# Edge rows for a 7x7 convolution: copied inside DRAM from the main rows instead of stored from the chip

## The chip, the core and the metric

The kernel runs on one core of a Trainium2 chip. A core has a matrix engine (TensorE, PE in the profile), a vector engine (VectorE, DVE), a scalar engine (ScalarE, ACT), a general engine (GpSimd, POOL) and a queue engine (SyncE, SP) that does little but issue transfers. The transfers themselves are moved by sixteen DMA engines that all queues share. The metric is the device time of one execution in microseconds (us), the median of several runs.

## What is computed

The input x has 384 channels of 192 x 192 numbers in float32. The reference is two layers:

```python
# layer 0
qkv = maxpool2x2(conv1x1(groupnorm(x), w_qkv))          # 1152 channels of 96 x 96
q, k, v = split(depthwise3x3(qkv))
attn = normalize(q) @ normalize(k).T * temperature      # 48 x 48 in each of 8 heads
out = sum(a_i * topk_softmax(attn, k_i) @ v)            # four values of k
x = x + conv1x1(upsample2x(gelu(out)), w_proj)
# layer 1
x = x + depthwise7x7(groupnorm(x), symmetrized weight)
```

The 7x7 convolution of layer 1 needs, for each output row, three rows above and three below it.

## The kernel before

The kernel runs in four stages: the statistics of the first norm, the q and k part with the sums for the attention matrix, the v part, and the 7x7 convolution. The change lies in the third, which also makes what the fourth reads.

**How the image is cut.** The 192 rows are six strips (`NT`) of 32 rows (`TR`). The v stage works on sixteen blocks (`NBC`); block b takes rows 2b and 2b+1 (`RB` = 2) of all six strips at once. The blocks are gone through in the order 13, 14, 15, 0, 1, 2 and so on (`order`, line 528), so that a block's neighbours are there in time.

**What the v stage leaves in DRAM.** The sum x + layer 0 is written channel by channel in a layout that suits the 7x7 stage: `sd` (line 115) has 4 x 32 rows of 384 channels, where a row is a run of 300 numbers (`RUN`): six strips of 50. The factor 4 (`CP`) splits the columns by their remainder modulo 4. `sh` (line 117) has 64 more rows of the same shape: the edge rows. For each of the three rows above and below a strip it holds ten shifted views (`NQ` = 10), which the 7x7 stage reads as further rows of its matrix product, 30 for above, 30 for below. Each edge row equals, but for a shift of a strip (50 numbers, `JP`) or of one column, a main row in `sd`: rows 29, 30 and 31 of the strip before, or rows 0, 1 and 2 of the strip behind.

**The loop of the v stage** (lines 1137 to 1164) runs for i = 3 to 15. One pass does, for v's block i, nine products `convolve` (line 542: six products of TensorE each, then a maximum on DVE), reading image rows `xv` that `load_v` (line 933) brings in three groups of three transfers on SyncE's queue; and for block j = i - 2 it finishes the depthwise taps, applies the attention (`attend`), projects (`project`, line 1031) and adds the input (`residual`, line 1062), whose image rows `xr` come through `load_r` (line 1054), three transfers on the same queue. The buffer `xvs` of image rows exists once: a group is loaded again when the last product that reads it is over, which gives each load a lead of most of a block. The order of the products and of most work on DVE is fixed by hand (`keep`); the order of the transfers on SyncE's queue is not, and is chosen when the program is built.

**The stores.** `residual` builds two rows of 128 channels in one of three buffers `sx`. For each of the two rows it issues on GpSimd's queue one store to `sd` (line 1117), and, if the row is one of the six that lie at a strip's edge, three stores to `sh` (line 1127: four, four and two of the ten views). Rows 29 to 31 and 0 to 2 come in blocks 14, 15, 0 and 1, that is in the passes i = 3 to 6: 9, 18, 18 and 9 stores.

**The 7x7 stage** reads `sd` and `sh` through `load_main` and `load_aux` (line 1257). Its first reads of `sh` are issued at 2173.5 us of the profile.

Of the kernel before, what the change touches and what calls it, by code (L numbers as in the profile page):

```python
# [14 lines left out]
C = 384  # L15
# [44 lines left out]
TR = 32  # L60
NT = HW // TR
CP = 4
NJ = HW // CP
JP = NJ + 2
RUN = NT * JP
HALO = KS // 2
NQ = CP + KS - 1
LEAD = JP + 2


TOP = 32
BOT = 64
# [5 lines left out]
RB = 2  # L78
# [4 lines left out]
CB = 8  # L83
# [3 lines left out]
def conv_preact_d2(  # L87
# [17 lines left out]
    nc = tc.nc  # L105
# [9 lines left out]
    sd = dram.tile([CP * TR, C, RUN], F32, name="sd")  # L115

    sh = dram.tile([SHR, C, RUN], F32, name="sh")
# [177 lines left out]
    with tc.tile_pool(name="stp", bufs=1) as stp, tc.tile_pool(name="xsp", bufs=5) as xsp:  # L295
# [149 lines left out]
        for b in [*range(NB - 2, NX, -2), NX, *reversed(range(NX))]:  # L445
            n = 2 if b > NX else 1
# [88 lines left out]
    def image_rows(ct, b, t0, nt):  # L535
        return bass.AP(
            x.tensor,
            x.offset + (ct * P * HW + t0 * TR + b * RB) * HW,
            [[HW * HW, P], [TR * HW, nt], [1, RB * HW]],
        )  # L540

    def convolve(i, t0, ct, xb, pin):
        b, rows = order[i], place(i)
        o = (2 * KT + ct) * P
        ps = pv.tile([P, UT, 512], F32, name=f"pv{b}_{t0}_{ct}", tag="pv")
        for u in range(UT):
            for kt in range(KT):
                pin(
                    nc.tensor.matmul(  # L549
                        ps[:, u, 0 : RB * HW], wq[:, kt, o : o + P], xb[:, u, kt, :],  # L550
                        start=(kt == 0), stop=(kt == KT - 1),
                    )
                )
        pin(
            nc.vector.tensor_reduce(  # L555
                rows[ct][:, 1 + t0 : 1 + t0 + UT, 1 : PS + 1],
                ps[:, :, 0 : RB * HW].rearrange("p u (a w b) -> p u w a b", a=2, b=2),
                AX.XY,
                ALU.max,
            )  # L560
        )

    with ExitStack() as bx:
# [55 lines left out]
        with tc.issue_after(loaded):  # L619
            for kt in range(KT):  # L620
                cs = slice(kt * P, (kt + 1) * P)
# [137 lines left out]
        for b in range(NB + 1):  # L759
# [11 lines left out]
            for ct in range(2 * KT + 1):  # L771
# [12 lines left out]
                if b > 0 and ct > 0:  # L784
# [5 lines left out]
                    flat = dst.rearrange("p h w -> p (h w)")  # L790
# [142 lines left out]
    def load_v(i, t0):  # L933
        xb = xvs[:, t0 : t0 + UT]
        for kt in range(KT):
            nc.sync.dma_start(xb[:, :, kt], image_rows(kt, order[i], t0, UT))
        return xb
# [4 lines left out]
    def depthwise_v(i, ct, dys, pin=lambda ins: ins):  # L942

        b = order[i % NBC]
        if (i, ct) not in vbs:
            tag = f"vlast{i}" if i >= NBC - 1 else "vb"
            vbs[i, ct] = vp.tile(
                [P, NT, PS], F32, name=f"vb{i}_{ct}", tag=tag, bufs=KT if i >= NBC - 1 else 2 * KT
            )
        dst = vbs[i, ct]  # L950
        for dy in dys:
            r = b + dy - 1
            t0 = 1 + r // NBC
            rows = place(i + dy - 1)[ct]
            for j in range(3):
                src = rows[:, t0 : t0 + NT, j : j + PS]
                w = wd[:, 2 * KT + ct, 3 * dy + j : 3 * dy + j + 1]
                if (i, ct) in begun:
                    pin(nc.vector.scalar_tensor_tensor(dst, src, w, dst, ALU.mult, ALU.add))  # L959
                else:  # L960
                    begun.add((i, ct))
                    pin(
                        nc.vector.tensor_scalar(
                            dst, src, w, bdb[:, 2 * KT + ct : 2 * KT + ct + 1], ALU.mult, ALU.add
                        )
                    )


    AHEAD = 3
# [55 lines left out]
    sdv = sd.rearrange("(v r) c n -> r c v n", v=CP)  # L1025
# [28 lines left out]
    def load_r(i, ot):  # L1054

        if i == NBC - 1:
            return xvs[:, :, ot]
        xr = xp2.tile([P, NT, RB * HW], F32, name=f"xr{order[i % NBC]}_{ot}", tag="xr")
        nc.sync.dma_start(xr, image_rows(ot, order[i % NBC], 0, NT))
        return xr  # L1060

    def residual(i, ot, y, xr, pin):

        b = order[i % NBC]
        flat = sxs[(i * KT + ot) % len(sxs)]
        xq = xr.rearrange("p t (a j e) -> p a t j e", a=RB, e=CP)

        def at(e):

            return LEAD + (e + CP - 1) % CP * RB * RUN + int(e > 0)  # L1070


        for e, f in ((1, 2), (0, 3)):
            for a in range(RB):
                pin(
                    nc.vector.tensor_tensor(  # L1076
                        bass.AP(
                            flat.tensor, flat.offset + at(e) + a * RUN,
                            [flat.ap[0], [JP, NT], [1, NJ], [at(f) - at(e), 2]],
                        ),  # L1080
                        xq[:, a, :, :, e : f + 1 : f - e],
                        y,
                        ALU.add,
                    )
                )
            yield
        if i == 1:

            m = mid1[:, ot : ot + 1]
            nc.vector.tensor_tensor(m, ysum[:, ot, b, 0:1], ysum[:, ot, b, 1:2], ALU.add)  # L1090
            nc.vector.tensor_scalar_mul(m, m, 1.0 / PBC)
            nc.vector.tensor_tensor(m, m, chmean[:, ot : ot + 1], ALU.add)
            nc.vector.tensor_scalar_mul(negmid[:, ot : ot + 1], m, -1.0)
        for k, (e, f) in enumerate(((1, 2), (3, 0))):
            pin(
                nc.scalar.activation(  # L1096
                    junk,
                    bass.AP(
                        flat.tensor, flat.offset + at(e),
                        [flat.ap[0], [at(f) - at(e), 2], [JP, RB * NT], [1, NJ]],  # L1100
                    ),
                    AF.Square, bias=negmid[:, ot : ot + 1], accum_out=sqsum[:, ot, b, k : k + 1],
                )
            )
            if k == 0:
                yield
        cs = slice(ot * P, (ot + 1) * P)

        def rows_of(a, nv, shift):
            o = LEAD + a * RUN + shift  # L1110
            return bass.AP(
                flat.tensor, flat.offset + o, [flat.ap[0], [RB * RUN, nv], [1, RUN]]
            )

        for a in range(RB):
            r = b * RB + a
            nc.gpsimd.dma_start(sdv[r, cs], rows_of(a, CP, 0))  # L1117

            halos = []
            if r >= TR - HALO:  # L1120
                halos.append(((r - TR + HALO) * NQ, -JP))
            if r < HALO:
                halos.append((BOT - TOP + r * NQ, JP))
            for h, shift in halos:
                for q in range(0, NQ, CP):
                    nv = min(CP, NQ - q)
                    nc.gpsimd.dma_start(
                        sh[h + q : h + q + nv, cs].rearrange("f c n -> c f n"),
                        rows_of(a, nv, shift + q // CP),
                    )  # L1130


    spare = [(NBC, ct, dy) for ct in range(KT) for dy in (1, 2)]
# [3 lines left out]
    for i in range(AHEAD, NBC):  # L1137
        j = i - 2
        xb = load_v(i, 0)
        for ct in range(KT):  # L1140
            depthwise_v(j, ct, (2,), keep)
            convolve(i, 0, ct, xb, keep)
        gl = attend(j)
        xb = load_v(i, UT)
        for ct in range(KT):
            depthwise_v(i - 1, ct, (0, 1), keep)
            if ct == 1:
                convolve(i, UT, 0, xb, keep)
        convolve(i, UT, 1, xb, keep)
        if spare[i - AHEAD]:  # L1150
            depthwise_v(*spare[i - AHEAD][:2], spare[i - AHEAD][2:], keep)
        convolve(i, UT, 2, xb, keep)
        ys = [project(j, ot, gl) for ot in range(KT)]
        xb = load_v(i, 2 * UT)
        sums = [residual(j, ot, ys[ot], load_r(j, ot), dve_keep) for ot in range(KT)]
        for ot in range(2):
            for _ in sums[ot]:
                pass
        convolve(i, 2 * UT, 0, xb, keep)
        next(sums[2])  # L1160
        convolve(i, 2 * UT, 1, xb, keep)
        for _ in sums[2]:
            pass
        convolve(i, 2 * UT, 2, xb, keep)
# [7 lines left out]
    for j in range(NBC - 2, NBC + 1):  # L1172
        gl = attend(j, keep)
        after = []
        for ot in range(KT):
            for _ in before[ot]:
                pass
            y = project(j, ot, gl, keep)
            after.append(residual(j, ot, y, load_r(j, ot), keep))
            next(after[ot])  # L1180
            next(after[ot])
            if (j, ot) == (NBC - 2, 1):
                for ct in range(KT):
                    depthwise_v(NBC, ct, (0,), keep)
        before = after
# [13 lines left out]
    with ExitStack() as ex_:  # L1199
# [258 lines left out]
        for n in range(steps):  # L1458
# [33 lines left out]
            for q in range(CP):  # L1492
                ps = sums(q, range(2 if q in ahead else 0, 3))
                c = n * CB + 2 * q
# [16 lines left out]
            if n in later:  # L1511
                ps = pc.tile([P, 2, 512], F32, name=f"al{later[n]}", tag="pc")
                for i, dg in enumerate(dgs):
                    cs = slice(i * P, (i + 1) * P)
# [63 lines left out]
```

## Time and profile before

The time is 2763.55 us, the median of 3 runs (2759.44 to 2763.87). The profiled execution took 2784.9 us at a mean granted TensorE clock of 0.985.

| engine | busy, us | share of the span |
|---|---|---|
| PE (products) | 2591.1 | 93% |
| PE weight loads, beside the products | 1525.2 | 55% |
| DVE | 2456.2 | 88% |
| ACT | 1140.1 | 41% |
| POOL | 746.7 | 27% |

| DMA queue | what it carries | MB | share of 16 engines |
|---|---|---|---|
| q1 (SyncE and others) | x, xv, xr, output | 283.44 | 29.0% |
| q0 (GpSimd) | sd, sh, weights of the 7x7 stage | 148.85 | 15.8% |
| q10 (ACT) | inputs of the 7x7 stage | 147.07 | 14.1% |

A share is an average over the whole span, while the stages differ much: the core's DMA moved 34 to 40 GB/s in parts of the q and k stage and 372 GB/s in most of the 7x7 stage. What a change in the v stage is worth must be read from that stage. It begins to load residual rows at 1360 us, its edge rows are stored from 1488.6 to 1679.2 us, and its last store to `sd` is issued at 2197 us. The page gives the time in 40 slices of 69.6 us; a finer table of stretches and the list of waits are shown with the prediction.

### The profile page before, as it was taken

The numbers are of one execution on the slowest core, as the hardware profiler recorded it, in microseconds if no ns is written. First come the engines' busy times: TensorE is split into PE (matmuls) and PEld (weight loads), VectorE is DVE, ScalarE is ACT, GpSimd is POOL, SyncE is SP. The second block draws the span as 40 slices with busy tenths as digits, with TensorE's granted clock in tenths as the row PEclk, the third lists the DMA queues.
The fourth block names the chain that finished last, engine by engine and source line by source line (L and its number), as shares of the span: only waits on it lengthen the run. The fifth ranks groups of instructions, "written<-read, shape, count | busy, mean of one in ns | idle before, by whom it ended". The sixth has DMA issues, their size and how long they took to land. (4 is left out here: it accounts for less than half of the span.)

```text
span 2784.9 us, 25837 instructions
## 1 busy us (share of the span) xinstructions
PE 2591.1 (93%) x8365; PEld 1525.2 (55%) x8365; DVE 2456.2 (88%) x3527; ACT 1140.1 (41%) x2262; POOL 746.7 (27%) x885
## 2 busy tenths in 40 slices
PE   0399999999999999999899969999999899999998
PEld 0144444444444444444556646666666677777776
DVE  7989998989999999999789958999889789888886
ACT  0143423333343333433402312232323577777776
POOL 1024443100000000000111321010101478787876
PEclk9999999999999999999899989999999999999999
DMA  9976766301010110110336997566674899999998
GB/s 381 402 252 217 249 213 228 130 34 68 35 68 35 40 62 35 68 35 0 120 103 238 340 362 231 192 230 219 203 246 151 324 343 366 372 375 372 372 374 264
DMA packets 234039, 581.01 MB, mean 209 GB/s; under 512 B 16640, under 2 KB 165744, under 8 KB 217136
## 3 DMA queue, kind: packets, MB, share of 16 engines
q1 hardware_dynamic: 173408, 283.44, 29.0%
q0 software_dynamic: 37376, 148.85, 15.8%
q10 hardware_dynamic: 23120, 147.07, 14.1%
q8 instruction: 67, 1.10, 0.2%
q14 instruction: 68, 0.56, 0.1%
HBM read 370.93 MB, written 208.21 MB: 208 GB/s over the span
## 5 line engine op out<-in xcount | busy, mean ns | idle before, releaser
L663 PE MATMUL pq<-xq,wq 128*128 128x512 f32 x2268 | 1028.8, 597 | 5.4 <-DVE ring L673 4.7
L708 DVE SCALAR_TENSOR_TENSOR qk<-ring,wd,qk 128x384 f32<-128x384 f32 x1152 | 699.4, 616 | 59.5 <-ACT ring L695 32.1
L663 PEld LDWEIGHTS pq<-xq,wq 128*128 128x128 f32 x2268 | 408.7, 190 | 437.3 <-issue 364.0
L549 PE MATMUL pv<-xv,wq 128*128 128x384 f32 x1656 | 545.7, 490 | 26.0 <-DMA xv<-in_x_dram 21.7
L549 PEld LDWEIGHTS pv<-xv,wq 128*128 128x128 f32 x1656 | 316.7, 192 | 245.8 <-issue 20.4
L1482 PE MATMUL pc<-main,w 128*128 128x288 f32 x1536 | 436.4, 406 | 3.0 <-PE al L1515 1.7
L1502 DVE TENSOR_SCALAR apart<-pc,rb 32x576 f32<-32x576 f32 x384 | 312.1, 813 | 81.2 <-PE pc L1482 55.4
L1482 PEld LDWEIGHTS pc<-main,w 128*128 128x128 f32 x1536 | 290.6, 190 | 87.1 <-issue 2.4
L725 ACT COPY qkT<-turns 32x288 f32<-32x288 f32 x768 | 329.0, 428 | 20.7 <-DVE turns L791 9.3
L1500 ACT ACTIVATE apart<-pc,rb 32x576 f32<-32x576 f32 x384 | 281.1, 732 | 133.5 <-PE pc L1482 128.7
L959 DVE SCALAR_TENSOR_TENSOR vb<-rows,wd,vb 128x576 f32<-128x576 f32 x384 | 313.3, 817 | 11.3
L673 DVE TENSOR_REDUCE ring<-pq 128x128 f32<-128x512 f32 x428 | 292.1, 683 | 3.7 <-PE pq L663 3.6
L1482 PE MATMUL pc<-aux,h 128*128 128x288 f32 x768 | 248.1, 405 | 0.0
L719 ACT ACTIVATE junk<-qk 128x384 f32<-128x384 f32 x144 | 71.1, 494 | 411.8 <-DVE qk L708 411.0
L1441 POOL COPY res<-apart 128x1152 f32<-128x1152 f32 (+1 forms) x96 | 222.0, 2338 | 13.3 <-ACT apart L1500 9.5
L826 POOL TENSOR_TENSOR rn<-rn,halfpos 128x6 f32<-128x6 f32 x1 | 1.4, 1359 | 827.5 <-DVE rn L825 827.5
L1076 DVE TENSOR_TENSOR sx<-xr,y 128x576 f32<-128x576 f32 x180 | 203.8, 1173 | 19.9 <-ACT y L1047 14.8
L555 DVE TENSOR_REDUCE rows<-pv 128x192 f32<-128x768 f32 x144 | 137.7, 957 | 84.7 <-PE pv L549 84.6
L1117 POOL DMA_DIRECT2D sd<-sx x96 | 72.2, 755 | 514.5 <-DVE sx L1076 493.2
L741 PEld LDWEIGHTS grams<-qkT,qkT 128*96 128x96 f32 x576 | 92.8, 165 | 147.3 <-issue 136.1
L1096 ACT ACTIVATE wq<-sx,negmid 128x1152 f32<-128x1152 f32 x96 | 120.6, 1257 | 122.5 <-DVE sx L1076 118.2
L1482 PEld LDWEIGHTS pc<-aux,h 128*128 128x128 f32 x768 | 145.1, 189 | 41.2 <-issue 0.2
(227 smaller groups left out, 2270.6 us busy)
## 6 DMA issues: line engine op xcount, KB each, us to landing
sd<-sx POOLq DMA_DIRECT2D x96, 600.0 KB, 10.1
out_dram<-res SPq DMA_DIRECT2D x192, 288.0 KB, 11.2
main<-sd ACTq DMA_DIRECT2D x46, 1200.0 KB, 6.7
xv<-in_x_dram SPq DMA_DIRECT2D x138, 384.0 KB, 6.6
xr<-in_x_dram SPq DMA_DIRECT2D x45, 1152.0 KB, 11.7
xq<-in_x_dram SPq DMA_DIRECT2D x21, 2304.0 KB, 8.2
w<-wt ACTq DMA_DIRECT2D x46, 1024.0 KB
xs<-in_x_dram SPq DMA_DIRECT2D x24, 1536.0 KB, 15.1
```

Of the source, the lines that this page charges most:

```text
L549: nc.tensor.matmul(ps[:, u, 0 : RB * HW], wq[:, kt, o : o + P], xb[:, u, kt, :], start=(kt == 0), stop=(kt == KT - 1),)
L555: nc.vector.tensor_reduce(rows[ct][:, 1 + t0 : 1 + t0 + UT, 1 : PS + 1], ps[:, :, 0 : RB * HW].rearrange("p u (a w b) -> p u w a b", a=2, ...
L663: ins = nc.tensor.matmul(ps, wq[:, kt, ct * P : (ct + 1) * P], rows[:, kt, :, g * 64 : (g + 1) * 64], start=(kt == 0), stop=(kt == KT - 1) ...
L673: nc.vector.tensor_reduce(t[:, r0 : r0 + PR, 1 + g * 32 : 1 + (g + 1) * 32], ps.rearrange("p (h a w b) -> p h w a b", h=PR, a=2, b=2), AX. ...
L708: nc.vector.scalar_tensor_tensor(dst, src, w, dst, ALU.mult, ALU.add)
L725: nc.scalar.copy(side[f * Q : (f + 1) * Q].rearrange("p c (t n) -> p t c n", n=P)[:, :, :, a * Q : (a + 1) * Q], turns[a * Q : (a + 1) * Q ...
L959: pin(nc.vector.scalar_tensor_tensor(dst, src, w, dst, ALU.mult, ALU.add))
L1076: nc.vector.tensor_tensor(bass.AP(flat.tensor, flat.offset + at(e) + a * RUN, [flat.ap[0], [JP, NT], [1, NJ], [at(f) - at(e), 2]],), xq[:, ...
L1441: keep(copy(res[ps, k], apart[ps, :, k].rearrange("p e n -> p n e")))
L1482: nc.tensor.matmul(ahead[q][:, k, 0 : NT * NJ], lhs, rhs, start=(j == 0), stop=(j == 2), skip_group_check=True,)
L1500: keep(nc.scalar.mul(dst, src, scale))
L1502: keep(nc.vector.tensor_scalar_mul(dst, src, scale))
```

## The change

The stores of edge rows (`rows_of` and the loop over `halos`) go. What is stored to `sd` stays as it is. A list `edges` has the 18 transfers that fill `sh`: six rows by three groups of views (4, 4 and 2). Each is a copy from `sd` to `sh` for all 384 channels, on SyncE's queue. `copy_edge` issues the next of them. It is called behind the three groups of `xv` loads of a pass, from pass i = 7 on: two in each pass and a third in odd passes, until the list is empty. The purpose is to take the edge rows out of the passes in which they are all made at once, and to spread them over later passes.

```diff
         cs = slice(ot * P, (ot + 1) * P)
-        def rows_of(a, nv, shift):
...
         for a in range(RB):
-            r = b * RB + a
-            nc.gpsimd.dma_start(sdv[r, cs], rows_of(a, CP, 0))
-
-            halos = []
-            if r >= TR - HALO:
-                halos.append(((r - TR + HALO) * NQ, -JP))
-            if r < HALO:
-                halos.append((BOT - TOP + r * NQ, JP))
-            for h, shift in halos:
-                for q in range(0, NQ, CP):
-                    nv = min(CP, NQ - q)
-                    nc.gpsimd.dma_start(
-                        sh[h + q : h + q + nv, cs].rearrange("f c n -> c f n"),
-                        rows_of(a, nv, shift + q // CP),
-                    )
+            nc.gpsimd.dma_start(
+                sdv[b * RB + a, cs],
...
+            )
+    edges = [
+        (f + h * NQ + q, r + h, shift + q // CP, min(CP, NQ - q))
+        for f, r, shift in ((0, TR - HALO, -JP), (BOT - TOP, 0, JP))
+        for h in range(HALO)
+        for q in range(0, NQ, CP)
+    ]
+
+    def copy_edge(now):
+        if not now or not edges:
+            return
+        f, r, shift, nv = edges.pop(0)
+        n = CB * RUN
+        nc.sync.dma_start(
+            sh[f : f + nv].rearrange("f (a c) n -> f a (c n)", c=CB),
+            bass.AP(
+                sd.tensor, sd.offset + r * C * RUN + shift,
+                [[TR * C * RUN, nv], [n, C // CB], [1, n]],
+            ),
+        )
...
         xb = load_v(i, 0)
+        copy_edge(i > AHEAD + 3)
...
         xb = load_v(i, UT)
+        copy_edge(i > AHEAD + 3)
...
         xb = load_v(i, 2 * UT)
+        copy_edge(i > AHEAD + 3 and i % 2)
```

More of the change, by code (lines that the diff above doesn't have):

```diff
@@ L1107, in residual @@
         cs = slice(ot * P, (ot + 1) * P)
-        def rows_of(a, nv, shift):
-            o = LEAD + a * RUN + shift
-            return bass.AP(
-                flat.tensor, flat.offset + o, [flat.ap[0], [RB * RUN, nv], [1, RUN]]
-            )
-        for a in range(RB):
-            r = b * RB + a
-            nc.gpsimd.dma_start(sdv[r, cs], rows_of(a, CP, 0))
-            halos = []
-            if r >= TR - HALO:
-                halos.append(((r - TR + HALO) * NQ, -JP))
-            if r < HALO:
-                halos.append((BOT - TOP + r * NQ, JP))
-            for h, shift in halos:
-                for q in range(0, NQ, CP):
-                    nv = min(CP, NQ - q)
-                    nc.gpsimd.dma_start(
-                        sh[h + q : h + q + nv, cs].rearrange("f c n -> c f n"),
-                        rows_of(a, nv, shift + q // CP),
-                    )
+        for a in range(RB):
+            nc.gpsimd.dma_start(
+                sdv[b * RB + a, cs],
+                bass.AP(
+                    flat.tensor, flat.offset + LEAD + a * RUN,
+                    [flat.ap[0], [RB * RUN, CP], [1, RUN]],
+                ),
+            )
+    edges = [
[11 more added lines that the diff above has]
+            sh[f : f + nv].rearrange("f (a c) n -> f a (c n)", c=CB),
+            bass.AP(
+                sd.tensor, sd.offset + r * C * RUN + shift,
+                [[TR * C * RUN, nv], [n, C // CB], [1, n]],
+            ),
+        )
     spare = [(NBC, ct, dy) for ct in range(KT) for dy in (1, 2)]
```

## The prediction

> **What bounds the kernel now.** I read the page first (section 2, then the sums of section 1), then the table of stretches, then who waited for whom, then the order of time around the one hole. The chain of waits is of no use here: it was followed only over the last microsecond or so before the end. Section 2 of the page, 40 slices of 69.6 us each:
>
> ```profile
> PE   0399999999999999999899969999999899999998
> DMA  9976766301010110110336997566674899999998
> ```
>
> TensorE (PE) is at nine tenths in all slices but a few, and the change lies in slices 21 to 31 (1460 to 2230 us), the stage that makes v, attends, projects and stores. There one slice falls to 6, number 23, right where the DMA row reads 9 9. So the stage is TensorE's except at one place. The stretches between the issues of the first residual load of each block show what a block costs (columns: length, then busy time of PE, weight loads, DVE, ACT and POOL, then clock, DMA share, GB/s):
>
> ```profile
> 1490.30:1539.60 49.30, 49.30 (x169) 31.84 (x169) 45.50 (x61) 15.00 (x32) 11.91 (x16) 1.00 0.92 315
> 1539.60:1589.00 49.40, 49.40 (x170) 31.94 (x169) 44.91 (x53) 13.76 (x30) 18.06 (x24) 1.00 1.02 356
> 1589.00:1660.70 71.70, 53.19 (x175) 33.01 (x173) 49.63 (x55) 18.77 (x40) 23.82 (x32) 0.87 1.03 364
> 1660.70:1714.50 53.80, 50.61 (x163) 32.38 (x164) 40.37 (x48) 8.76 (x20) 3.70 (x5) 0.92 0.65 214
> 1714.50:1763.90 49.40, 49.40 (x170) 31.94 (x169) 45.01 (x52) 13.77 (x30) 4.48 (x6) 1.00 0.66 219
> ```
>
> An undisturbed block is 49.4 us of unbroken TensorE, with the DMA engines at 0.65 and 219 GB/s. While edge rows are stored the DMA share rises to 1.0. The third and fourth stretch together are 125.5 us, which is 26.7 us over two blocks. That is all that the edge stores cost today. What ended the waits from 1440 to 1720 us (total, times, longest):
>
> ```profile
> PE pv L549 <- DMA xv<-in_x_dram: 21.7, 3, 15.9
> ```
>
> So TensorE stood 21.7 us for image rows whose loads queued behind saturated DMA; the other 5 us are the lower clock after the stand (0.87 and 0.92). The DMA answer gives the transfers of one block and those to be replaced (KB each, median us to landing):
>
> ```profile
> sd<-sx POOLq DMA_DIRECT2D x96, 600.0 KB, 10.1
> xv<-in_x_dram SPq DMA_DIRECT2D x138, 384.0 KB, 6.6
> xr<-in_x_dram SPq DMA_DIRECT2D x45, 1152.0 KB, 11.7
> sh<-sx POOLq DMA_DIRECT2D x36, 600.0 KB, 16.2
> sh<-sx POOLq DMA_DIRECT2D x18, 300.0 KB, 16.0
> ```
>
> [...] an xv load, 6.6 us at the median, needed up to 38.6 us while the Pool queue was full of stores.
>
> **The change, part by part.**
>
> 1. 54 stores of edge rows leave the Pool queue (36 of 600 KB, 18 of 300 KB: 27.65 MB). On Pool they are 54 x 0.75 us = 41 us of issue, worth nothing: Pool is 27% busy and waits for DVE. On the DMA engines they are 27.65 MB at the 367 GB/s that the saturated window 1580 to 1630 us shows, 75 us of all sixteen, in four blocks. The middle two carried 10.8 + 9.2 = 20 MB each, 54 us of DMA in a block of 49.4. Their removal takes away the hole: **minus 26.7 us**.
>
> 2. 18 copies join the SyncE queue, in which all xv and xr loads of this stage stand. The source asks for 4 (or 2) rows of 48 pieces, but the built instruction carries a pattern of 4 x 8 x 14400 numbers (2 x 8 x 14400 for the six small ones): slowest dimension 4 or 2. [...] Either way each of these moves 460.8 KB: one whole row of 384 x 300 numbers. [...]
>
> 3. Cost of one copy on such an engine. No DRAM to DRAM transfer of this size is in the trace. Nearest row: the page's best slice moved 402 GB/s, 25.1 GB/s an engine: 460.8 KB take 18.3 us. [...] For the upper end I let reading and writing the same memory cost 20% more, 22 us (an estimate). I take 18.3 us: 18 x 18.3 = 330 us.
>
> 4. Where they lie. In the changed program's order of instructions the copies stand behind the xv groups, over nine blocks: 1, 1, 1, 2, 3, 2, 3, 2, 3. The first ones are moved ahead of the eighth block, since they are not pinned. Base traffic of an engine in a block: 219 GB/s x 49.4 us = 10.8 MB, at 367 GB/s 29.4 us (at the best slice's 402 it is 26.8; by the share of 0.65, 32.1). Nine blocks have 445 us. Engine 0 then needs 9 x 29.4 + 330 = 594 us: **149 us too many**.
>
> 5. What of it is hidden. A load has a lead: the xv group issued at 1803.8 us is used one block less one group later, at 1842.7 (its predecessor starts at 1793.3, plus 49.4). Of these 39 us a load needs some 7 to land, so about 30 us of backlog stay hidden, once. [...] On TensorE's path: 149 - 30 = **119 us**, in the blocks with two and three copies: such a block takes 29.4 + 36.6 = 66 or 29.4 + 54.9 = 84 us, in place of 49.4.
>
> 6. Waits that are added. A copy waits for the stores of its row in the main buffer; these were issued a block or more earlier and land in 10 us, so nothing. SyncE also waits, before each issue, for its transfer eight places earlier (the program rotates eight semaphores); behind a slow copy this holds xv and xr back, and through them TensorE and, by the pinned order, DVE. I count it inside item 4, as the same backlog. In the changed order the three xr loads stand behind the last xv group and, in odd blocks, behind a third copy; they start some 12 us later than now and lose as much of their lead. This is not priced apart either; it pushes upward.
>
> 7. At nothing: the reader of the edge rows in the last stage (first at 2173 us; the last copy is issued three blocks before the stage ends); the copies' issue time on SyncE (0.37 us for a load now); the extra 27.65 MB of DRAM reads (218 GB/s of the core's traffic is far from 402).
>
> Sum: 119 - 26.7 = +92 us; 2763.55 + 92 = **2856 us**.
>
> **The rivals.**
>
> (a) The copies are spread over all sixteen engines after all, because what the hardware is given differs from the pattern I read. Then a large copy is 1.84 MB at 402 GB/s, 4.6 us, three of them (one is small) 11.5 us, beside 17 us that are free in each block (0.35 x 49.4). Nothing stalls and the hole is gone: 2763.55 - 26.7 = 2737 us. For it: bytes alone fit with ease. Against it: the dimension of 4 in the instruction.
>
> (b) Copying inside DRAM runs at half the rate of a load: 36.7 us each, 660 us in all. 264 + 660 - 445 - 30 - 27 = +422: about 3190 us. Nothing in the profile speaks for it but the absence of such a transfer.
>
> (c) Four engines, but the loads behind the copies are not held[...]. Gain and loss would then roughly cancel: about 2763 us. [...]
>
> **How the numbers follow.** Forecast 0.76, (a) 0.14, (b) 0.08, (c) 0.02. [...] The high end is the slow price with the heavy base: 18 x 22 + 9 x 32.1 - 445 - 30 - 26.7 = +183, so 2947; I stretch it to 2985 for the xr loads' lost lead, the lower clock after each stand, and the near part of (b). That leaves out (a), (c) and most of (b), some 2 in 10. Faster 0.14, same 0.02, slower 0.84.
>
> **What would show it.** Right: landing of the sh<-sd copies near 20 us or above although four of them would fit in that time by bytes; TensorE's waits for xv loads (and DVE's for xr) of over 100 us, in the six blocks from about 1690 us on; blocks of 66 and 84 us in turn; a mean DMA share that stays under 0.7 while TensorE stands, because twelve engines idle. The stretch from 1589 to 1714.5 us back to 2 x 49.4 shows item 1. Wrong: copies that land in 5 to 8 us and blocks of 49.4 us throughout would be (a); landings near 40 us, (b). The prediction fails first if the number of engines isn't four and two.

## The result, and the profile after

The kernel with copies takes 2867.98 us (median of 4 runs, 2864.16 to 2876.64) against 2763.71 us before: a ratio of 1.0384, 95% interval 1.0357 to 1.041. It is 104 us slower; 92 were forecast.

The two rows of section 2 of the page after, in slices of 71.7 us:

```profile
PE   0399999999999999997999999686979899999998
DMA  9976666210101010101346666565565899999998
```

There is no hole left where the edge rows used to be stored, at 1600 us. In its place TensorE falls to 6, 8, 6, 9, 7, 9 in slices 25 to 30 (the first slice is number 0), and just there the DMA row stays at 5 or 6. TensorE waits for transfers while the DMA engines are, on average, nearly half idle.

The table of stretches after, each from the first product of `attend` to that of the next block (length, then busy PE, weight loads, DVE, ACT, POOL, then clock, DMA share, GB/s):

```profile
1709.60:1759.00 49.40, 49.40 (x170) 31.98 (x169) 44.99 (x51) 14.01 (x30) 4.49 (x6) 1.00 0.68 247
1759.00:1835.30 76.30, 52.62 (x170) 33.14 (x169) 44.34 (x51) 14.11 (x30) 4.48 (x6) 0.84 0.54 194
1835.30:1896.80 61.50, 54.51 (x170) 33.73 (x169) 44.41 (x51) 14.12 (x30) 4.50 (x6) 0.92 0.60 218
1896.80:1975.80 79.00, 54.05 (x170) 33.63 (x169) 44.36 (x51) 14.11 (x30) 4.49 (x6) 0.85 0.54 194
1975.80:2037.40 61.60, 54.76 (x169) 33.83 (x168) 42.41 (x48) 14.12 (x30) 4.50 (x6) 0.92 0.61 220
2037.40:2116.10 78.70, 54.75 (x169) 34.00 (x168) 42.32 (x48) 14.11 (x30) 4.48 (x6) 0.83 0.61 213
2116.10:2165.50 49.40, 49.40 (x169) 31.96 (x168) 42.71 (x48) 13.77 (x30) 4.49 (x6) 1.00 0.72 246
```

Five blocks are stretched, by 76.3 + 61.5 + 79.0 + 61.6 + 78.7 - 5 x 49.4 = 110 us, long and short in turn as the copies come three and two to a pass. Of these 110 us TensorE stood 86.4; in the rest its products took longer, 270.7 us where five undisturbed blocks take 247.0, at a granted clock of 0.83 to 0.92. Three windows cut out of one stretched block, same columns, make the point sharper:

```profile
1774.20:1782.00 7.80, 7.80 (x30) 5.42 (x29) 5.35 (x7) 1.18 (x4) 0.00 (x0) 1.00 0.26 111
1794.30:1802.00 7.70, 0.00 (x0) 0.00 (x0) 0.00 (x0) 0.00 (x0) 0.00 (x0) 0.78 0.12 52
1794.00:1807.00 13.00, 0.17 (x1) 0.00 (x0) 0.00 (x0) 0.00 (x0) 0.00 (x0) 0.68 0.34 121
```

In the third window no compute engine works for 13 us, but for 0.17 us of TensorE: DVE waits for xr, until 1807.2 us, and the others for DVE. The first two windows hold nothing but pieces of a copy. In the trace's DMA records, one for each piece that an engine moves, four pieces are under way throughout the first and two throughout the second, and the shares, 0.26 and 0.12, are about four and two engines of sixteen. So the numbers four and two can be read from the trace; which engines they are it does not say, and 0 and 1 in the forecast and the expectations are names only. Over the whole profile never more than four pieces of copies are under way at once, but for under 1 us where one ends as another begins.

Who waited for transfers, or for one who did, from 1440 to 2330 us (total, times, longest):

```profile
DVE sx L1076 <- DMA xr<-in_x_dram: 96.6, 5, 27.5
...
PE pv L549 <- DVE rows L555: 71.2, 5, 22.8
...
PE pv L549 <- DMA xv<-in_x_dram: 15.2, 9, 2.0
```

Most of the stand begins on DVE: its addition of x (line 1076) lacks the xr rows. The order on DVE is pinned, so the maxima of `convolve` stand behind the addition, their sums stay in the matrix engine's output buffers, and TensorE waits for DVE (the second line). The rest is TensorE's own wait for xv. The copies themselves need no more than expected: in the DMA records a piece of 57.6 KB takes 2.13 us (median of 480), 27.1 GB/s, so the 460.8 KB on one engine take 17.0 us.

### The profile page after: what moved, and what is told of

It reads as the page before. It is cut to its first block, busy times and chain, and to the rows that moved or that the text cites. A ratio compares the mean times of both kernels' runs of the same rounds, so it can differ in the third digit from the quotient of the medians.

```text
span 2867.1 us, 25774 instructions
## 1 busy us (share of the span) xinstructions
PE 2612.0 (91%) x8365; PEld 1535.3 (54%) x8365; DVE 2439.7 (85%) x3527; ACT 1142.7 (40%) x2262; POOL 706.8 (25%) x831
## 5 line engine op out<-in xcount | busy, mean ns | idle before, releaser
L549 PE MATMUL pv<-xv,wq 128*128 128x384 f32 x1656 | 565.8, 503 | 90.6 <-DVE rows L555 75.4
L549 PEld LDWEIGHTS pv<-xv,wq 128*128 128x128 f32 x1656 | 324.6, 197 | 322.3 <-DVE rows L555 79.7
L1076 DVE TENSOR_TENSOR sx<-xr,y 128x576 f32<-128x576 f32 x180 | 203.2, 1170 | 108.7 <-DMA xr<-in_x_dram 96.6
```

Source lines behind the costliest of these rows:

```text
L549: nc.tensor.matmul(ps[:, u, 0 : RB * HW], wq[:, kt, o : o + P], xb[:, u, kt, :], start=(kt == 0), stop=(kt == KT - 1),)
L1076: nc.vector.tensor_tensor(bass.AP(flat.tensor, flat.offset + at(e) + a * RUN, [flat.ap[0], [JP, NT], [1, NJ], [at(f) - at(e), 2]],), xq[:, ...
```

## The experiments

Theory 1 is the prediction's: a copy runs on as many engines as the slowest dimension of its pattern allows, the same two to four get every copy, and what they must do no longer fits. Theory 2: copying inside DRAM is slow or disturbs the loads on whatever engines. Theory 3: the loads of xr merely stand behind copies in the queue. Ratios are to the kernel before, run on the same chip.

### The same pieces on eight engines, and on sixteen

```diff
-            sh[f : f + nv].rearrange("f (a c) n -> f a (c n)", c=CB),
+            sh[f : f + nv].rearrange("f (a c) n -> a f (c n)", a=8),      # or a=16
...
-                [[TR * C * RUN, nv], [n, C // CB], [1, n]],
+                [[C * RUN // 8, 8], [TR * C * RUN, nv], [1, C * RUN // 8]],
```

> The same 18 copies at the same places on the same queue, in the same pieces of 57.6 KB; only the two outer dimensions of the pattern are swapped, so that the slowest is 8 (8 x 4 x 14400, 8 x 2 x 14400) instead of 4 or 2. Theory 1 (the copies run on as many engines as the slowest dimension allows, and two of them get too much): each of eight engines now carries 12 x 230 KB + 6 x 115 KB = 3.5 MB, 127 us at 27.1 GB/s, in nine blocks that have 20 us to spare each; no block is stretched, about 2760 us. Theory 2 (copying inside DRAM is slow or disturbs the loads whatever engines it runs on): nothing changes, about 2868 us. Theory 3 (the loads of xr come too late because copies stand before them in the queue): they still do, so between the two, 2830 us or more.

> As before with the slowest dimension 16 (16 x 4 x 7200, 16 x 2 x 7200): all sixteen engines, pieces of 28.8 KB. Theory 1: 64 us of copying on each engine over nine blocks, about 2760 us, at most 5 us from the version on eight engines. Theory 2: about 2868 us. Theory 3: 2830 us or more.

Measured: 2761.98 us on eight (ratio 0.9996, 0.998 to 1.0012), 2760.06 us on sixteen (0.9998, 0.9988 to 1.0007). The whole loss is gone by a change of the order of two dimensions; with eight, even the pieces (57.6 KB, 2.13 us) are the same. The stretches with eight engines, columns as above:

```profile
1756.90:1806.30 49.40, 49.40 (x170) 31.94 (x169) 44.76 (x51) 14.01 (x30) 4.49 (x6) 1.00 0.83 309
1806.30:1855.70 49.40, 49.40 (x170) 31.94 (x169) 44.75 (x51) 13.99 (x30) 4.50 (x6) 1.00 0.78 278
```

Blocks of 49.4 us with more bytes per microsecond than in any stretched block. And in the DMA records of the first version eight pieces of copies are mostly under way at once (97 us in all), in those of the second up to sixteen (28 us). Theories 2 and 3 both fall: the bytes, the place and the number of copies did not change.

### Twice the load on the two engines

Each copy of four rows is issued as two of two rows.

```diff
-        nc.sync.dma_start(
-            sh[f : f + nv].rearrange("f (a c) n -> f a (c n)", c=CB),
+        for v in range(0, nv, 2):
+            nc.sync.dma_start(
+                sh[f + v : f + v + 2].rearrange("f (a c) n -> f a (c n)", c=CB),
...
-                [[TR * C * RUN, nv], [n, C // CB], [1, n]],
+                    [[TR * C * RUN, 2], [n, C // CB], [1, n]],
```

> The same bytes at the same places, but each copy of four rows is issued as two copies of two rows, all with the slowest dimension 2: 30 copies, each with 460.8 KB on each of engines 0 and 1, none on others. Theory 1: 30 x 17.0 us = 510 us on these two, against 9 x 20 us of free time and the hidden lead of 15 to 30 us, so 300 us on the path: 3040 to 3090 us. Theory 2 (the bytes copied inside DRAM count, not the engines): 2868 us as now. Theory 3 (place in the queue, number of copies): somewhat over 2868 us, under 2950.

Measured: 3073.2 us (ratio 1.1135, 1.1116 to 1.1154), inside theory 1's 3040 to 3090. Its stretches:

```profile
1825.80:1938.50 112.70, 56.29 (x170) 34.36 (x169) 44.33 (x51) 14.11 (x30) 4.48 (x6) 0.74 0.37 137
1938.50:2016.80 78.30, 56.30 (x169) 34.43 (x168) 44.39 (x51) 14.11 (x30) 4.50 (x6) 0.85 0.47 170
```

Passes with five and with three such copies. In this profile two pieces are under way at once (462 us in all), and a third for less than 1 us, so copies that stood in the queue together did not run on different engines. Together with the blocks of the changed kernel one line fits: block = 27.7 us + 17.0 us x copies. That gives 61.7 and 78.7 for two and three (measured 61.5 and 61.6; 79.0, 78.7 and here 78.3) and 112.7 for five; only the first long block of the changed kernel is shorter, 76.3. The 17.0 us are the eight pieces of 2.13 us. The 27.7 us agree with an estimate from the DMA records: in a block each engine has on average 288 pieces of loads at 65 ns and 48 pieces of `sd` stores at 194 ns (medians), together 28.0 us. And with more work on the two engines the mean share is lower: 0.37 and 0.47, where the changed kernel had 0.54 to 0.61.

### One copy in each pass

```diff
+    edges = edges[::2]
...
         xb = load_v(i, UT)
-        copy_edge(i > AHEAD + 3)
...
-        copy_edge(i > AHEAD + 3 and i % 2)
```

The filling with zeros that stands in for the other nine is shown further below.

> Nine of the 18 copies, one in each pass, still on four or two engines; the rows of the other nine are filled with zeros in the q and k stage, so that the output leaves their share out. Theory 1: a copy of 17 us fits in the 20 us that engine 0 has free in each block, no stretch, 2750 to 2762 us. Theory 2 and 3: half of the loss remains, about 2815 us.

Measured: 2755.22 us (0.9979, 0.9972 to 0.9987), and the profile has 49.4 us for each block. A copy a block on these engines was hidden, as 27.7 + 17.0 = 44.7 < 49.4 says. Not half of the loss remains, but none. (The 0.2% below the kernel before is taken up with the filling.)

### Copies behind the loads of xr

```diff
-        copy_edge(i > AHEAD + 3)
...
         sums = [residual(j, ot, ys[ot], load_r(j, ot), dve_keep) for ot in range(KT)]
+        for _ in range(2 + i % 2):
+            copy_edge(i > AHEAD + 3)
```

> The 18 copies as they are, but called behind the loads of xr of a pass instead of between the loads of xv, so that no xr load has a copy of its own pass right ahead. Theory 1: engines 0 and 1 have the same work, the wait only moves from xr to xv: 2850 to 2885 us. Theory 3: the 97 us that DVE waited for xr disappear, 2760 to 2800 us.

Measured: 2883.93 us (1.0457, 1.0435 to 1.0478). DVE's wait for xr is gone, and this line stands in the list of waits instead:

```profile
PE pv L549 <- DMA xv<-in_x_dram: 97.4, 18, 22.3
```

The name of the wait changed, its size not much: TensorE stood 71.2 + 15.2 = 86.4 us before and 97.4 now. Six blocks are stretched here, to 420 us together, and the whole is 16 us longer. It would have been a mistake to read the first list as "xr comes too late" and to mend the order of the queue.

### The same copies on ScalarE's queue

```diff
-        nc.sync.dma_start(
+        nc.scalar.dma_start(
             sh[f : f + nv].rearrange("f (a c) n -> f a (c n)", c=CB),
```

> The 18 copies as they are (four or two engines), but issued on ScalarE's queue[...]. Theory 1: engines 0 and 1 still have 594 us of work in 445 us[...], so the stretch stays, 2830 to 2900 us. Theory 3 (only the place in the queue): the stretch goes, about 2760 us. [...]

Measured: 2935.16 us (1.0633, 1.0606 to 1.0659), worse than on the loads' own queue and above the range of theory 1. TensorE's wait is again for xv, and DVE waits for ScalarE, 75.4 us where it was 7.2:

```profile
PE pv L549 <- DMA xv<-in_x_dram: 131.1, 15, 35.0
DVE sx L1076 <- ACT y L1047: 75.4, 15, 15.5
```

In the profile six blocks are stretched, to 477 us together. By the same line six blocks and all 18 copies are 6 x 27.7 + 18 x 17.0 = 472 us. A queue of its own did not add an engine: in the DMA records again never more than four pieces are under way at once, but for 0.1 us. The copies start earlier and crowd into six blocks (the last one is issued at 1937 us instead of 2042), so less of the free time of later blocks is used. ScalarE, on whose queue the copies now are, also stood for transfers (its three longest waits for them were 47.3, 28.7 and 27.0 us); how much of the extra 67 us is its stand and how much the crowding was not separated.

### The same copies on GpSimd's queue

```diff
-        nc.sync.dma_start(
+        nc.gpsimd.dma_start(
             sh[f : f + nv].rearrange("f (a c) n -> f a (c n)", c=CB),
```

> The 18 copies as they are (patterns 4 x 8 x 14400 and 2 x 8 x 14400), issued on GpSimd's queue. [...] Theory 1a (what hurts is that the same two to four engines get every copy): [...] single copies hide in the lead: 2755 to 2790 us. Theory 1b (any copy on four engines holds back the loads for its length): [...] 2850 us or more.

Measured: 2760.13 us (0.9996, 0.9985 to 1.0007), all blocks at 49.4 us, with patterns whose slowest dimension is still 4 or 2. The transfers in the page of this run (KB each, us to landing):

```profile
sd<-sx POOLq DMA_DIRECT2D x96, 600.0 KB, 9.7
xv<-in_x_dram SPq DMA_DIRECT2D x138, 384.0 KB, 8.1
xr<-in_x_dram SPq DMA_DIRECT2D x45, 1152.0 KB, 11.3
sh<-sd POOLq DMA_DIRECT2D x12, 1800.0 KB, 26.5
sh<-sd POOLq DMA_DIRECT2D x6, 900.0 KB, 26.4
```

A copy of half the bytes lands after the same 26 us, which fits half as many engines for it; spread over sixteen, the landings were 12.3 and 10.1 us. But from 1440 to 2160 us neither TensorE nor DVE waits for an xv or xr load here. So a copy on few engines did no harm by itself, as in the run with one copy in each pass (49.4 us a block); what cost time was the same few every time (2868 us). The DMA records show the difference: in this run up to ten pieces of copies are under way at once (36 us in all), as many as two large copies and a small one side by side would give, where the same copies on SyncE's and ScalarE's queues never went beyond four but for those overlaps. So different copies did run on different engines here, which before the run was the author's assumption. In which order they take them is not shown: the trace doesn't number the engines.

### What the edge stores cost before

Three runs bear on the 26.7 us. The kernel before, profiled again; the kernel without any edge rows in this stage; and the whole kernel before with only the filling that the former needs:

```diff
+            if 3 <= b < 21:
+                f0, kt0 = divmod(b - 3, KT)
+                f0 = f0 * NQ if f0 < HALO else BOT - TOP + (f0 - HALO) * NQ
+                nc.sync.dma_start(
+                    sh[f0 : f0 + NQ, kt0 * P : (kt0 + 1) * P].rearrange("f c n -> c f n"),
+                    z[:, RUN : 2 * RUN].unsqueeze(1).to_broadcast([P, NQ, RUN]),
+                )
```

> The kernel before once more with a profile. If the hole of 26.7 us belongs to this kernel whenever it is profiled, the profile shows it again and takes about 2785 us; if it was a rare event, the profile has blocks of 49.4 us throughout and takes 2750 to 2770 us like the other executions.

> Neither edge stores nor copies in the v stage; the edge rows are filled once with zeros in the q and k stage, whose DMA is nearly idle, so the output leaves the edge rows' share out. This gives the floor: what the edge stores of the kernel before cost in time. If the hole of 26.7 us that the profile of before shows is there in every execution, 2737 us. If it belongs to the profiled execution (2786.7 us, against 2759 to 2766 in the others), 2755 to 2762 us.

> The kernel before, complete with its edge stores, plus the filling with zeros in the q and k stage that the version without edge rows has. If that version's 0.24% comes from leaving out the edge stores, this one is at 2758 to 2764 us; if it comes from the filling's effect on the earlier stages, it is at 2752 to 2756 us too, and the edge stores of before cost nothing measurable.

The second profile of the kernel before took 2757.2 us, not 2784.9, and its stretches in the first three blocks with edge stores are these:

```profile
1506.30:1555.70 49.40, 49.40 (x170) 31.93 (x169) 45.00 (x52) 13.78 (x30) 11.90 (x16) 1.00 0.89 316
1555.70:1605.10 49.40, 49.40 (x170) 31.94 (x169) 44.76 (x52) 13.77 (x30) 18.69 (x25) 1.00 1.04 390
1605.10:1654.50 49.40, 49.24 (x167) 31.17 (x166) 44.10 (x50) 13.79 (x30) 16.97 (x23) 1.00 1.04 387
```

Saturated as before, but at 387 to 390 GB/s where the first profile had 356 to 364, the same stores just fit. The longest block of that profile is 50.3 us, 0.9 us of loss; with the filling the same block is 53.3 us, 3.9 us of loss. Without edge rows the kernel takes 2753.67 us (0.9976, 0.9967 to 0.9986), with edge stores and the filling 2756.51 us (0.9987, 0.9977 to 0.9997). Both fell outside the ranges expected for them: the first 1.3 us below 2755 to 2762, the second between its two ranges. The difference of some 3 us is the best figure for what the edge stores cost; the intervals overlap, so it may be nothing. Why the DMA moved less in the first profile, and by what the filling shortens the earlier stages, was not settled.

## Why the prediction was right, and where its steps were off

**The number of engines (item 2): right,** and shown twice, by the order of two dimensions (2762 against 2868 us) and by the four and two pieces under way in the DMA records. Before the run it was the author's assumption, which the trace before did not show. It carried the forecast: rival (a) counted the same bytes and came out on the other side. Its number (2737 us) was not reached by the versions on eight and sixteen engines either, for the reason in the next point.

**The gain (item 1): mis-sized.** 26.7 us were taken from one profile. The three runs of the kernel before that stood beside it, 2759 to 2764 us, already said that the profiled execution of 2784.9 us was not like them; the forecast read the hole and did not set the two numbers side by side. What it measured: 0.9 us in a second profile, some 3 us in the comparison without edge rows. By the forecast's count the stores and loads of a block with 18 stores asked for 54 us of DMA in 49.4 at 367 GB/s; at 390 they need 51. That the lead of the loads covers the rest fits, but was not shown.

**The copy (item 3): 17.0 us instead of 18.3.** The best slice of the page gave 25.1 GB/s an engine; the pieces here moved at 27.1. The 20% more that the upper end allowed for reading and writing the same memory was not needed, and rival (b), half the rate, is out. 18 copies: 306 us instead of 330.

**The base traffic (item 4): 27.7 us a block instead of 29.4,** by the line through the stretched blocks. The forecast blocks of 66 and 84 us were 61.6 and 78.7.

**What is hidden (item 5): half of it, or less.** By the line, the six blocks with two and three copies ask for 6 x 27.7 + 15 x 17.0 = 421 us, 125 more than 6 x 49.4. 110 were lost, so 15 us of lead were hidden, not 30. The forecast took the lead of an xv load; the loads that came late were those of xr (96.6 us of waiting on DVE). And with the copies behind the xr loads the same 15 copies took 420 us of the 421, so hardly anything was hidden there. Besides, three blocks with one copy left 4.7 us each unused, which the sum over nine blocks had counted as available.

Sum: 119 forecast on the path and 110 measured; 26.7 forecast as gain and 1 to 3 measured. That makes 107 to 109, and the medians say 104, with an interval of 99 to 113. So +92 is near +104 in part by luck: the first term is right to a tenth, the second was too large by a factor of nine or more, and the total hides that. The 119 is helped by luck too. The prices of items 3 and 4 were 39 us too high (24 and 15), and the hidden and the unused time 29 us the other way (15 and 14).

**Waits and order (item 6): right that they add little of their own.** Moving copies behind the xr loads changed which load was late and moved the time by 16 us (2884 against 2868 us). **The signs** held in the main: waits for xv and xr of 112 us together (15.2 and 96.6), blocks long and short in turn, five of them from 1759 us on where six from 1690 were named, and a mean share of 0.54 to 0.61 in them. Only the landing of these copies couldn't be read: the trace of the changed kernel gives none for them.

## What to carry to other kernels

Count a transfer's cost on the engine that carries most of it (here 17.0 us a copy), not as bytes over sixteen: look at the outermost dimension of the pattern as built, since neighbouring dimensions may have been merged and split anew (here 48 x 2400 became 8 x 14400, pieces of 57.6 KB), and put a longer one outermost (on SyncE's queue 8 and 16 cost nothing here, 4 and 2 cost 104 us). The sign of it here was compute engines that waited while the mean DMA share was 0.54 to 0.61; the wait's name, xr or xv, only told who stood last in the line. And before a hole in a profile is booked as a gain, compare the profiled execution's time with the other runs.

## What was not expected of the hardware

Moving the copies to a second hardware queue made things worse, 2935 against 2868 us, where loads no longer stood behind copies in one queue. And the rate of saturated DMA in the same blocks of the same kernel was 356 to 364 GB/s in one execution, which lost 26.7 us there, and 387 to 390 in another, which lost 0.9.
